# Graph attention and convolution on one core: attention in blocks of a whole pair of heads, with six numerator tiles and an 8-bit mask

## The chip, the cores and the metric

The program runs on one core of one Trainium2 chip. The metric is the device time of that core in microseconds (us). Before the change the median of three runs is 2978.34 us (2978.21 to 2978.59); the profiled execution has a span of 2975.7 us.

## The reference: what is computed

The input `x` holds 32 batches of 512 nodes with 512 features; `adj` is a 512x512 matrix of zeros and ones. Two layers follow each other, each added to its input and normalised per node. The first is attention with 8 heads of 64 features, in which node i sees node j only where `adj` is not zero; the second is a graph convolution with a normalised adjacency.

```python
q = (x @ Wq + bq).reshape(b, n, H, HD)          # the same for k and v
scores = jnp.einsum('bihd,bjhd->bhij', q, k) / jnp.sqrt(jnp.float32(HD))
mask = jnp.where(adj == 0, jnp.float32(-1000000000.0), jnp.float32(0.0))
weights = jax.nn.softmax(scores + mask[None, None, :, :], axis=-1)
out = jnp.einsum('bhij,bjhd->bihd', weights, v)
x = _layernorm(x + out)
norm_adj = adj * deg_inv_sqrt[:, None] * deg_inv_sqrt[None, :]
x = _layernorm(x + norm_adj @ (x @ weight) + bias)
```

## The kernel before, in words

**Attention.** The heads are taken in four pairs g, in the order (0, 2, 1, 3). A step (b, g, jj) handles two of the four 128-row blocks of keys of one pair. `scores` (line 337) multiplies, for each of its two blocks, the keys of both heads with the queries (64 rows of the array per head) into a tile `sc` of PSUM, of which there are two. VectorE then clips and adds the mask (`scalar_tensor_tensor`, line 348) and writes the numerator tile `e`; ScalarE takes its exponential in place (line 351); GpSimd adds the exponentials into `acc`, from which the softmax's denominators come: one addition for jj = 0 and two for jj = 1 (lines 363 to 368). `values` (line 370) multiplies the `e` tiles of a step with the values into `av`, 64 columns of the array per head; after jj = 1 VectorE transposes `av` into `yb` and a DMA puts it into `yT`. `sums` (line 401) adds up `acc` over the partitions on TensorE.

**What runs between.** All other matmuls of a batch are cut into pieces. `seven` (line 250) builds a 1024-wide product from seven pieces of eight matmul instructions each: `values_of` (v0 to v6 below), `keys_and_queries` for r = 0 and r = 1 (q0 to q6, p0 to p6) and, for the second layer, `second` (s0 to s6). `first` makes the four products with the adjacency (f0 to f3). Each piece takes one of three PSUM buffers of `ps_mm`, and VectorE or ScalarE reads it out. Beside them are pieces without matmuls, of cost 0 in the list: `add` (VectorE multiplies a row block of `yT` by the inverse of the denominators, then GpSimd adds the residual), `measure` (VectorE, mean and variance), `root` (GpSimd), `judge` (VectorE), `norm` and `grow` (ScalarE), `split` (VectorE, then GpSimd), `turn` (VectorE transposes x), `combine` (GpSimd, for `xT` and for `parts` of the second layer), `store`.

**The order of the work.** It is written out by hand: every engine gets its instructions in program order (class `InOrder`). The main loop (line 681) runs over steps: scores of step k, values of step k-1, then a share of a list called `side`, made anew per batch at the batch's third step. With eight steps per batch the list of 32 pieces is cut in eighths, four pieces each. For batches 1 to 29 the list is built at lines 696 to 708: the sums' inverse first, then the chain of attention's layer norm (`add`, `measure`, `root`, `judge`, `norm`, `split`, `grow`) woven with what is left of the second layer's norm (`rest`), spread over the pieces v1 to p4; then f0 to f3, `combine` of `parts`, p5, p6, and s0 to s6. `weave` spreads one list over another in equal portions; `run` takes pieces off the front until their cost reaches the share that is due.

So each engine's queue in one eighth is: two score tiles, two value tiles, four pieces on TensorE; two masks, sometimes `yb`, then the pieces' read-outs on VectorE; one or two `acc` additions and then the side list's additions on GpSimd.

Of the kernel before, what the change touches and what calls it, by code (L numbers as in the profile page):

```python
# [8 lines left out]

F32 = mybir.dt.float32  # L10
I32 = mybir.dt.int32
BF16 = mybir.dt.bfloat16
F32R = mybir.dt.float32r
AF = mybir.ActivationFunctionType
ALU = mybir.AluOpType
AX = mybir.AxisListType

P = 128
H = 8
HD = 64  # L20
EPS = 1e-5
MASKED = -1e9
TINY = 1.1754943508222875e-38


CUT = 60.0
# [21 lines left out]
def unshifted(  # L48
# [29 lines left out]
    B, N, D = x.shape  # L78
    NT = N // P
    DT = D // P  # L80
    G = H // 2
# [21 lines left out]
    def load_x(b, j):  # L103


        if b == 0 and j == 1:
            X[b, j] = work.tile([P, 8, DT, 32], F32, name="x1", tag="e", bufs=4)
        else:
            X[b, j] = acts.tile([P, 8, DT, 32], F32, name="x", bufs=1)
        for q in range(4):  # L110
            nc.sync.dma_start(
                X[b, j][32 * q : 32 * (q + 1)],
                x[b, ts(j, HALF), ts(q, P)].rearrange("(k s) (t r) -> s k t r", s=32, r=32),
            )
# [85 lines left out]
    for c in range(2):  # L200
        gpsimd.memset(sel[:, c, c : c + 1], 1.0)
    FINE = consts.tile([P, B], F32, name="fine")
    maskT = consts.tile([P, NT, N], BF16, name="maskT")
    adjT = consts.tile([P, NT, N], F32R, name="adjT")
    dis = consts.tile([P, NT], F32, name="dis")
    lost = consts.tile([P, NT], F32, name="lost")
# [1 line left out]
    def adjacency(m):  # L208


        p = ps_mm.tile([P, N], F32, name="mm")
        for n in range(NT):
            tensor.transpose(p[:, ts(n, P)], adj_sb[:, n, ts(m, P)], ident)
        vector.tensor_scalar(maskT[:, m, :], p, 0.0, MASKED, op0=ALU.is_equal, op1=ALU.mult)
        vector.tensor_copy(adjT[:, m, :], p)
        off = work.tile([P, N], F32, name="off", tag="e", bufs=4)
        vector.tensor_tensor(off, p, adjT[:, m, :], ALU.not_equal)
        vector.tensor_reduce(lost[:, m : m + 1], off, AX.X, ALU.add)

# [117 lines left out]
    def scores(s):  # L337

        b, g, jj = s
        E[s] = [work.tile([P, 2, N], F32, name="e", bufs=4) for _ in range(2)]  # L340
        for l in range(2):
            j = 2 * jj + l
            e = E[s][l]
            p = ps_sc.tile([P, 2, N], F32, name="sc")
            for k in range(2):
                r = slice(k * HD, (k + 1) * HD)
                tensor.matmul(p[:, k, :], KQ[b, g][r, 0, ts(j, P)], KQ[b, g][r, 1, :], start=True, stop=True)
            vector.scalar_tensor_tensor(
                e, p, CUT, maskT[:, j, None, :].to_broadcast([P, 2, N]), op0=ALU.min, op1=ALU.add
            )  # L350
            scalar.activation(e, e, AF.Exp)
        if b == B - 1:

            n = 2 * ORDER.index(g) + jj
            if n == 3:
                a = XT[:, 4:6].rearrange("p k u o -> p k (u o)")
            elif n == 4:
                a = acts.tile([P, 2, N], F32, name="acc4", tag="kq", bufs=5)
            else:
                a = work.tile([P, 2, N], F32, name="acc", bufs=3)  # L360
            ACC.setdefault((b, g), []).append(a)
            gpsimd.tensor_add(a, E[s][0], E[s][1])
        elif jj == 0:
            ACC[b, g] = [work.tile([P, 2, N], F32, name="acc", bufs=3)]
            gpsimd.tensor_add(ACC[b, g][0], E[s][0], E[s][1])
        else:
            for l in range(2):
                gpsimd.tensor_add(ACC[b, g][0], ACC[b, g][0], E[s][l])
# [32 lines left out]
    def sums(b, c):  # L401


        p = ps_mm.tile([P, N], F32, name="mm")
        for q in range(4):
            parts = ACC[b, ORDER[2 * c + q // 2]]
            for k, a in enumerate(parts):
                tensor.matmul(
                    p[32 * q : 32 * (q + 1), :], sel[:, c, :], a[:, q % 2, :],
                    start=k == 0, stop=k == len(parts) - 1,  # L410
                )
        if c == 0:
            SM[b] = work.tile([P, N], F32, name="sT", bufs=1)
            if b < B - 1:
                scalar.copy(SM[b], p)
            else:
                vector.tensor_scalar(SM[b], p, 1e-36, None, op0=ALU.max)
        else:
            vector.scalar_tensor_tensor(SM[b], p, 1e-36, SM[b], op0=ALU.max, op1=ALU.add)
# [111 lines left out]
    def weave(side, main):  # L531

        out, done = [], 0
        for k, piece in enumerate(main):
            due = len(side) * (k + 1) // len(main)
            out += side[done:due] + [piece]
            done = due
        return out + side[done:]
# [109 lines left out]
    def run(pieces, share=1.0):  # L648

        due = share * sum(c for c, _, _ in pieces)  # L650
        done = 0
        while pieces and (done < due or share == 1.0):
            c, f, args = pieces.pop(0)
            f(*args)
            done += c

    ORDER = (0, 2, 1, 3)
    steps = [(b, g, jj) for b in range(B) for g in ORDER for jj in range(2)]
    S = len(steps)
    PER = 2 * G  # L660
    weigh(wv, gpsimd)
    run(sum(turns(0), []))
    weigh(wk, gpsimd)
# [14 lines left out]
    one, two = turns(1)  # L678
    run(one)
    side, rest, held = [], [], None  # L680
    for k in range(S + 2):
        b, at = divmod(k, PER)
        if at == 2:
            run(side)
            if b:
                load_residual(b - 1)
            if b + 2 < B:
                load_x(b + 2, 0)
            if b + 1 < B:
                main, kq = values_of(b + 1) + keys_and_queries(b + 1, 0), keys_and_queries(b + 1, 1)  # L690
                turn0, turn1 = turns(b + 2) if b + 2 < B else ([], [])
                main += kq[:2] + turn0 + kq[2:5]
            if b == 0:
                w1_parts = [(0, weigh_part, (w1, gpsimd, i)) for i in range(4)]
                side = main[:7] + [(0, degrees, ())] + weave(w1_parts, main[7:]) + kq[5:] + turn1
            elif b < B - 1:
                f, c = finish(b - 1), convolve(b - 1)
                norm, split, grow = f["norm"], f["split"], f["grow"]
                chain = f["add"][:1] + rest[:3] + f["add"][1:3] + rest[3:5] + f["add"][3:] + f["measure"][:1] + rest[5:]
                chain += f["measure"][1:] + f["root"] + f["judge"] + norm[:2] + split[:1] + norm[2:3] + split[1:2]  # L700
                chain += norm[3:] + split[2:] + grow
                side = f["inverse"] + main[:1] + weave(chain, main[1:])
                side += c["first"] + c["parts"][:2] + kq[5:6] + c["parts"][2:3] + kq[6:] + turn1[:1]
                if b < B - 2:
                    s = c["second"]
                    side += s[:1] + c["parts"][3:] + s[1:3] + turn1[1:2] + s[3:4] + turn1[2:3] + s[4:5] + turn1[3:4]
                    side += s[5:6] + c["measure"][:1] + turn1[4:] + s[6:] + c["measure"][1:2]
                    rest = c["measure"][2:] + c["root"] + c["store"]
                else:
                    side += c["parts"][3:]  # L710
                    held = c
            else:
                f, c = finish(b - 1), convolve(b - 1)
                s, norm, split = held["second"], f["norm"], f["split"]
                side = s[:1] + f["inverse"] + s[1:2] + f["add"][:2] + s[2:3] + f["add"][2:] + s[3:4] + f["measure"][:2]
                side += s[4:5] + f["measure"][2:] + f["root"] + s[5:6] + f["judge"] + held["measure"][:2] + s[6:]
                spread = norm[:2] + held["measure"][2:3] + split[:1] + norm[2:3] + held["measure"][3:] + split[1:2]
                spread += held["root"] + norm[3:] + split[2:] + held["store"]
                side += [(0.5, *piece[1:]) for piece in spread] + c["first"] + c["parts"] + f["grow"]
        if k >= 2:  # L720
            pb, pg, pj = steps[k - 2]
            if pj == 1 and pg in ORDER[1::2]:
                sums(pb, ORDER.index(pg) // 2)
        if k < S:
            scores(steps[k])
        if k == 0:
            run(two)
        if 1 <= k <= S:
            values(steps[k - 1])
        if k == S - 4:  # L730
            load_residual(B - 1)
            last = finish(B - 1)
        if k == S - 1:
            run(last["early"])
        run(side, 1.0 / (PER - (at - 2) % PER))
    run(side)

    f, e = last, convolve(B - 1)
    s, norm, split, block, add = c["second"], f["norm"], f["split"], e["block"], f["late"][1:]
# [308 lines left out]
```

## Time and profile before

| | busy us | share of the span | instructions |
|---|---|---|---|
| TensorE matmul | 2910.5 | 98% | 12966 |
| VectorE | 2110.8 | 71% | 2908 |
| ScalarE | 1064.8 | 36% | 1342 |
| GpSimd | 1827.4 | 61% | 1141 |

The largest groups of the profile, with the number of instructions and the mean duration: the mask on VectorE, 512 of 1217 ns; the exponential on ScalarE, 512 of 1057 ns; additions into `acc` on GpSimd, 248 of 2457 ns (onto `acc`) and 131 of 2438 ns (of two `e` tiles); score matmuls, 2048 of 618 ns; value matmuls, 2048 of 609 ns. The durations of matmuls overlap each other, so the distance from one start to the next says more than a duration. A busy share of 98% on TensorE means that a matmul is nearly always in flight, not that every start follows the last as soon as it could. A "wait" names the engine whose instruction came last before the waiting one could start. Idle time of an engine that doesn't set the end costs nothing.

### The profile page before, as it was taken

The numbers are of one execution on the slowest core, as the hardware profiler recorded it, in microseconds if no ns is written. First come the engines' busy times: TensorE is split into PE (matmuls) and PEld (weight loads), VectorE is DVE, ScalarE is ACT, GpSimd is POOL, SyncE is SP. The second block draws the span as 40 slices with busy tenths as digits, with TensorE's granted clock in tenths as the row PEclk, the third lists the DMA queues.
The fourth block names the chain that finished last, engine by engine and source line by source line (L and its number), as shares of the span: only waits on it lengthen the run. The fifth ranks groups of instructions, "written<-read, shape, count | busy, mean of one in ns | idle before, by whom it ended". The sixth has DMA issues, their size and how long they took to land.

```text
span 2975.7 us, 35550 instructions
## 1 busy us (share of the span) xinstructions
PE 2910.5 (98%) x12966; PEld 1865.2 (63%) x12966; DVE 2110.8 (71%) x2908; ACT 1064.8 (36%) x1342; POOL 1827.4 (61%) x1141
## 2 busy tenths in 40 slices
PE   7999999999999999999999999999999999999997
PEld 5666666666666666666666666666666666666645
DVE  6667766677666777666777667776667766677766
ACT  1233323343333433333433333433344333333333
POOL 2656666666666566666666665666666666666655
PEclk9999999999999999999999999999999999999998
DMA  5111121212112111211121121112111211121111
GB/s 128 33 25 47 47 57 39 49 40 54 47 47 49 41 46 47 57 39 44 44 56 47 46 47 43 46 47 55 41 40 46 57 46 47 46 43 47 42 40 51
DMA packets 383399, 142.41 MB, mean 48 GB/s; under 512 B 280048, under 2 KB 349680, under 8 KB 383216
## 3 DMA queue, kind: packets, MB, share of 16 engines
q1 hardware_dynamic: 381920, 138.75, 19.6%
q8 instruction: 104, 1.70, 0.2%
q10 hardware_dynamic: 1296, 1.31, 0.2%
q14 instruction: 79, 0.65, 0.1%
HBM read 72.88 MB, written 33.55 MB: 36 GB/s over the span
## 4 chain that ended last, share of the span: by engine, by line
PE 66%; DVE 17%; POOL 7%; issue 6%; DMA 1%; ACT 1%; SPq 0%; DVEq 0%; POOLq 0%; ACTq 0%
PE mm L42 44%; PE sc L42 12%; PE av L42 10%; DVE e L42 6%; POOL acc L42 5%; DVE yT L42 3%; DVE st L42 2%; DVE y L42 2%; DVE v L42 1%; POOL xT L42 1%; ACT e L42 1%; POOL y L42 1%; DMA xr<-in_x_dram 1%; DVE u L42 1%; DVE yb L42 1%
## 5 line engine op out<-in xcount | busy, mean ns | idle before, releaser
L42 ACT ACTIVATE e<-e 128x1024 f32<-128x1024 f32 x512 | 541.2, 1057 | 1230.7 <-DVE e L42 1211.7
L42 POOL TENSOR_TENSOR acc<-acc,e 128x1024 f32<-128x1024 f32 x248 | 609.2, 2457 | 400.2 <-ACT e L42 390.5
L42 DVE SCALAR_TENSOR_TENSOR e<-sc,maskT 128x1024 f32<-128x1024 f32 x512 | 601.8, 1217 | 111.5 <-PE sc L42 99.4
L42 POOL TENSOR_TENSOR acc<-e 128x1024 f32<-128x1024 f32 x131 | 319.4, 2438 | 408.0 <-ACT e L42 408.0
L42 PE MATMUL sc<-kq 64*128 64x512 f32 x2048 | 512.0, 618 | 5.4 <-DVE e L42 5.4
L42 PE MATMUL av<-e,v 128*64 128x512 f32 x2048 | 499.6, 609 | 5.2 <-DVE yb L42 3.5
L42 PE MATMUL mm<-xT,wk 128*128 128x256 f32 x1792 | 475.4, 388 | 23.1 <-DVE e L42 22.2
L42 PE MATMUL mm<-xT,wq 128*128 128x256 f32 x1792 | 460.0, 379 | 0.0
L42 PEld LDWEIGHTS mm<-xT,wk 128*128 128x128 f32 x1792 | 327.9, 190 | 174.6 <-DVE e L42 51.1
L42 PE MATMUL mm<-wv,xT 128*128 128x256 f32 x1792 | 405.8, 384 | 12.8 <-DVE xT L42 10.8
L42 PEld LDWEIGHTS mm<-wv,xT 128*128 128x128 f32 x1792 | 338.7, 192 | 84.1 <-DVE u L42 22.7
L42 PEld LDWEIGHTS mm<-xT,wq 128*128 128x128 f32 x1792 | 341.0, 190 | 45.4
L42 PEld LDWEIGHTS av<-e,v 128*64 128x64 f32 x2048 | 124.9, 137 | 348.3 <-issue 339.2
L42 PEld LDWEIGHTS sc<-kq 64*128 64x128 f32 x2048 | 177.0, 187 | 246.5 <-issue 233.2
L42 DVE TENSOR_TENSOR kq<-u,mm 128x512 f32<-128x512 f32 x128 | 87.8, 686 | 250.8 <-PE mm L42 247.8
L42 PE MATMUL mm<-w,zT 128*128 128x256 f32 x1024 | 232.4, 380 | 0.6 <-DVE zT L42 0.6
L42 DVE TENSOR_TENSOR yT<-yT,inv 128x512 f32<-128x512 f32 (+1 forms) x140 | 230.1, 1669 | 0.1
L42 PEld LDWEIGHTS mm<-w,zT 128*128 128x128 f32 x1024 | 194.3, 190 | 28.8 <-DVE zT L42 1.0
L42 PE MATMUL mm<-adjT,hi 128*128 128x512 f32 x496 | 205.1, 413 | 0.0
L42 POOL TENSOR_TENSOR yT<-yT,b_r 128x512 f32<-128x512 f32 x128 | 188.2, 1490 | 25.3 <-DVE lo L42 25.3
L42 PE MATMUL mm<-adjT,lo 128*128 128x512 f32 x496 | 196.5, 396 | 0.8 <-DVE lo L42 0.8
L42 DVE TENSOR_TENSOR y<-y,mm 128x512 f32<-128x512 f32 x160 | 106.0, 680 | 125.6 <-POOL y L42 75.7
(103 smaller groups left out, 3112.1 us busy)
## 6 DMA issues: line engine op xcount, KB each, us to landing
x<-in_x_dram SPq DMA_DIRECT2D x256, 128.0 KB, 3.0
yT<-yb SPq DMA_DIRECT2D x512, 64.0 KB, 2.5
out_dram<-y SPq DMA_DIRECT2D x128, 256.0 KB, 2.1
xr<-in_x_dram SPq DMA_DIRECT2D x124, 256.0 KB, 3.4
wv<-in_L_gnn_Wv_dram ACTq DMA_DIRECT2D x8, 128.0 KB, 5.0
wk<-in_L_gnn_Wk_dram SPq DMA_DIRECT2D x8, 128.0 KB, 4.2
wq<-in_L_gnn_Wq_dram SPq DMA_DIRECT2D x8, 128.0 KB, 4.7
yT<-in_adj_dram SPq DMA_DIRECT2D x1, 1024.0 KB, 6.8
```

Source lines behind the costliest of these rows:

```text
L42: return self.tc.keep_in_program_order(op(*args, **kwargs))
```

## The change

It has four parts.

1. The loop runs over blocks of a whole pair of heads (four per batch) in place of half pairs. In a block TensorE makes the scores of the pair's first half, then all values of the pair in front, then (in every second block) `sums`, then the scores of the second half, and then a quarter of the side list in one go. The additions into `acc` are taken out of `scores` into `accumulate`: that of the first half comes after `sums`, those of the second half after its scores.
2. Six numerator tiles `e` in place of four, since four of a pair are kept while two of the next are made. Two `acc` tiles in place of three, and other spare places for the last batch.
3. The mask is kept as bytes, 255 where there is no edge, and subtracted; before it was 16-bit, -1e9, and added. The score is clipped at 60, so a masked numerator is exp of at most -195, zero in 32 bits. This frees the room for part 2.
4. The chain of attention's layer norm comes later in the side list: `rest` is woven over the first five pieces, and the chain, with the inverse, over the fifteen that follow.

```diff
-        E[s] = [work.tile([P, 2, N], F32, name="e", bufs=4) for _ in range(2)]
+        E[s] = [work.tile([P, 2, N], F32, name="e", bufs=6) for _ in range(2)]
...
-                e, p, CUT, maskT[:, j, None, :].to_broadcast([P, 2, N]), op0=ALU.min, op1=ALU.add
+                e, p, CUT, maskT[:, j, None, :].to_broadcast([P, 2, N]), op0=ALU.min, op1=ALU.subtract
...
-                chain = f["add"][:1] + rest[:3] + f["add"][1:3] + rest[3:5] + f["add"][3:] + f["measure"][:1] + rest[5:]
-                chain += f["measure"][1:] + f["root"] + f["judge"] + norm[:2] + split[:1] + norm[2:3] + split[1:2]
-                chain += norm[3:] + split[2:] + grow
-                side = f["inverse"] + main[:1] + weave(chain, main[1:])
+                chain = f["inverse"] + f["add"] + f["measure"] + f["root"] + f["judge"] + norm[:2] + split[:1]
+                chain += norm[2:3] + split[1:2] + norm[3:] + split[2:] + grow
+                side = weave(rest, main[:5]) + weave(chain, main[5:])
...
-        if k >= 2:
-            pb, pg, pj = steps[k - 2]
-            if pj == 1 and pg in ORDER[1::2]:
-                sums(pb, ORDER.index(pg) // 2)
         if k < S:
-            scores(steps[k])
+            scores((*blocks[k], 0))
+        if k:
+            values((*blocks[k - 1], 0))
+            values((*blocks[k - 1], 1))
+            if k % 2 == 0:
+                sums(blocks[k - 1][0], (k - 1) % G // 2)
+        if k < S:
+            accumulate((*blocks[k], 0))
+            scores((*blocks[k], 1))
+            accumulate((*blocks[k], 1))
         if k == 0:
             run(two)
-        if 1 <= k <= S:
-            values(steps[k - 1])
...
-        run(side, 1.0 / (PER - (at - 2) % PER))
+        run(side, 1.0 / (G - (at - 1) % G))
```

More of the change, by code (lines that the diff above doesn't have):

```diff
@@ L11 @@
 I32 = mybir.dt.int32
-BF16 = mybir.dt.bfloat16
+U8 = mybir.dt.uint8
 F32R = mybir.dt.float32r
@@ L22 @@
 MASKED = -1e9
+FAR = 255.0
 TINY = 1.1754943508222875e-38
@@ L106, in load_x @@
         if b == 0 and j == 1:
-            X[b, j] = work.tile([P, 8, DT, 32], F32, name="x1", tag="e", bufs=4)
+            X[b, j] = work.tile([P, 8, DT, 32], F32, name="x1", tag="e", bufs=6)
         else:
@@ L202, in unshifted @@
     FINE = consts.tile([P, B], F32, name="fine")
-    maskT = consts.tile([P, NT, N], BF16, name="maskT")
+    maskT = consts.tile([P, NT, N], U8, name="maskT")
     adjT = consts.tile([P, NT, N], F32R, name="adjT")
@@ L213, in adjacency @@
             tensor.transpose(p[:, ts(n, P)], adj_sb[:, n, ts(m, P)], ident)
-        vector.tensor_scalar(maskT[:, m, :], p, 0.0, MASKED, op0=ALU.is_equal, op1=ALU.mult)
+        vector.tensor_scalar(maskT[:, m, :], p, 0.0, FAR, op0=ALU.is_equal, op1=ALU.mult)
         vector.tensor_copy(adjT[:, m, :], p)
-        off = work.tile([P, N], F32, name="off", tag="e", bufs=4)
+        off = work.tile([P, N], F32, name="off", tag="e", bufs=6)
         vector.tensor_tensor(off, p, adjT[:, m, :], ALU.not_equal)
@@ L348, in scores, with accumulate @@
             vector.scalar_tensor_tensor(
-                e, p, CUT, maskT[:, j, None, :].to_broadcast([P, 2, N]), op0=ALU.min, op1=ALU.add
+                e, p, CUT, maskT[:, j, None, :].to_broadcast([P, 2, N]), op0=ALU.min, op1=ALU.subtract
             )
             scalar.activation(e, e, AF.Exp)
+    def accumulate(s):
+        b, g, jj = s
+        n = 2 * ORDER.index(g) + jj
+        a = None
         if b == B - 1:
[L354 to L360, printed above, removed]
+            if n in (2, 6, 7):
+                a = XT[:, 0:2] if n == 7 else XT[:, 4:6]
+                a = a.rearrange("p k u o -> p k (u o)")
+            elif n == 3:
+                a = acts.tile([P, 2, N], F32, name="acc3", tag="kq", bufs=5)
+        if a is None and (jj == 0 or b == B - 1):
+            a = work.tile([P, 2, N], F32, name="acc", bufs=2)
+        if a is not None:
             ACC.setdefault((b, g), []).append(a)
             gpsimd.tensor_add(a, E[s][0], E[s][1])
-        elif jj == 0:
-            ACC[b, g] = [work.tile([P, 2, N], F32, name="acc", bufs=3)]
-            gpsimd.tensor_add(ACC[b, g][0], E[s][0], E[s][1])
         else:
@@ L657, in unshifted @@
     ORDER = (0, 2, 1, 3)
-    steps = [(b, g, jj) for b in range(B) for g in ORDER for jj in range(2)]
-    S = len(steps)
-    PER = 2 * G
+    blocks = [(b, g) for b in range(B) for g in ORDER]
+    S = len(blocks)
     weigh(wv, gpsimd)
@@ L680, in unshifted @@
     side, rest, held = [], [], None
-    for k in range(S + 2):
-        b, at = divmod(k, PER)
-        if at == 2:
+    for k in range(S + 1):
+        b, at = divmod(k, G)
+        if at == 1:
             run(side)
@@ L719, in unshifted @@
                 side += [(0.5, *piece[1:]) for piece in spread] + c["first"] + c["parts"] + f["grow"]
-        if k >= 2:
-            pb, pg, pj = steps[k - 2]
-            if pj == 1 and pg in ORDER[1::2]:
-                sums(pb, ORDER.index(pg) // 2)
         if k < S:
-            scores(steps[k])
+            scores((*blocks[k], 0))
[8 more added lines that the diff above has]
+            accumulate((*blocks[k], 1))
         if k == 0:
             run(two)
-        if 1 <= k <= S:
-            values(steps[k - 1])
-        if k == S - 4:
+        if k == S - 2:
             load_residual(B - 1)
@@ L734, in unshifted @@
             run(last["early"])
-        run(side, 1.0 / (PER - (at - 2) % PER))
-    run(side)
+        run(side, 1.0 / (G - (at - 1) % G))
     f, e = last, convolve(B - 1)
```

## The prediction, before the result was known

> **What bounds the kernel now.** I read the page first, for the engine that sets the end.
>
> ```profile
> PE 2910.5 (98%) x12966; PEld 1865.2 (63%) x12966; DVE 2110.8 (71%) x2908; ACT 1064.8 (36%) x1342; POOL 1827.4 (61%) x1141
> PE 66%; DVE 17%; POOL 7%; issue 6%; DMA 1%; ACT 1%; SPq 0%; DVEq 0%; POOLq 0%; ACTq 0%
> ```
>
> TensorE (PE) is nearly never without a matmul. Next, its own waits: only one repeats, 29 times, once per full batch.
>
> ```profile
> PE mm L42 <- DVE e L42: 24.2, 29, 2.0
> ```
>
> The third view is the timeline of TensorE in mid-run (start, length of the group, name):
>
> ```profile
> 1527.01 1.99 PE L42 MATMUL sc<-kq 64*128 64x512 f32 x8
> 1528.93 1.94 PE L42 MATMUL av<-e,v 128*64 128x512 f32 x8
> 1530.79 1.13 PE L42 MATMUL mm<-xT,wk 128*128 128x256 f32 x4
> 1531.76 1.03 PE L42 MATMUL mm<-xT,wq 128*128 128x256 f32 x4
> 1532.62 1.03 PE L42 MATMUL mm<-xT,wk 128*128 128x256 f32 x4
> ...
> 1537.90 1.06 PE L42 MATMUL mm<-acc,sel 128*32 128x512 f32 x8
> ```
>
> From 1531.76 to 1532.62 four matmuls take 0.864, so 0.216 each, 1.728 per piece of eight. The four pieces from 1530.79 to 1537.90 take 7.10, not 32 x 0.216 = 6.91: 0.19 is lost. Scores run in pairs of starts 0.43 apart, so 4 x 0.43 = 1.72, but values start 1.92 after scores: 0.20 lost. Values to the next group: 1.87, 0.15 lost. Each turn scores, values, pieces loses 0.54 to three changes of the array's shape (64*128, 128*64, 128*128).
>
> The fourth view shows what the other engines do to each other: VectorE (DVE) and GpSimd (POOL) around the repeating wait.
>
> ```profile
> 1518.05 2.35 DVE L42 SCALAR_TENSOR_TENSOR e<-sc,maskT 128x1024 f32<-128x1024 f32 x2
> 1520.32 3.46 DVE L42 TENSOR_TENSOR yT<-yT,inv 128x512 f32<-128x512 f32 x2
> 1523.69 0.68 DVE L42 TENSOR_TENSOR v<-u,mm 128x512 f32<-128x512 f32 x1
> 1524.29 0.68 DVE L42 TENSOR_TENSOR e<-e,mm 128x512 f32<-128x512 f32 x1
> 1520.49 5.49 POOL L42 TENSOR_TENSOR acc<-acc,e 128x1024 f32<-128x1024 f32 x2 [2.31 <-ACT e L42]
> 1525.11 1.10 PE L42 MATMUL mm<-xT,wk 128*128 128x256 f32 x4 [0.79 <-DVE e L42]
> ```
>
> Two multiplications of `add` need 3.46: the first 0.6, the second only after GpSimd's first addition to acc. v4's read-out comes late (1524.97), its PSUM buffer is wanted by q0 at 1518.87 + 0.10 + 3 x 1.728 = 1524.15, and q0 starts at 1525.11: 0.95 lost per batch.
>
> **The Trainium skill.** "TensorEngine Tiling (Array Packing)", Key Properties, says that changing the tiling mode, not just the tile, drains TensorE. The trace agrees: 0.15 to 0.20 at each change, none within a mode. "SBUF — State Buffer", Who interferes with whom, says that a VectorE instruction with two SBUF inputs contends with GpSimd's reads, and one with a single SBUF input does not. The trace agrees: `add` took up to 2.86 us beside acc and 0.68 without, while the mask (scores in PSUM) stays at 1.14 from start to start.
>
> **The change, part by part.**
>
> *Blocks of a pair: fewer changes of shape.* Before, a pair had 2 x (pieces to scores + scores to values + values to pieces). Entry and exit can be told apart by the first start-to-start time of a group: pieces enter 0.10 late (1530.79 to 1531.76 is 0.97, not 0.864) and leave 0.09 late; scores enter 0.10 late (their weight loads at 1503.81 and 1504.34 lie 0.53 apart, not 0.43) and leave 0.10 late; values 0.05 and 0.10. So, to three places, 0.197, 0.148 and 0.204; a pair pays 1.098. After: pieces to scores 0.197, scores to values 0.148, values to scores, scores to pieces. The trace has no undisturbed values-to-scores; I bound it by the cheapest and dearest change, 0.148 to 0.204, and take 0.198 (exit 0.094 to 0.10, entry of scores 0.104). Scores to pieces: exit 0.097 + entry 0.104 = 0.201. Sum 0.744; saved 0.354 (0.348 to 0.398), times 128 pairs 45.3 us. `inverse`'s transposes (shape of the pieces) stood right behind values and paid the entry there; in mid-list they save nothing: 31 x 0.1 = 3.1 back. Saving 42.2.
>
> *The old wait goes.* The adds now come after v5, behind which acc is long done: 29 x 0.95 = 27.6 saved.
>
> *Longer runs, and both acc additions in front.* Cutting the list (67.8 of cost; 2.1 per piece, 0.6 the inverse) in quarters gives: Q1 v0-v4, inverse, v5, add0, add1, v6, add2, q0; Q2 add3, m0, q1, m1, q2, m2, m3, q3, root, q4, judge, q5, q6, split0, p0, split1, p1 (norms between); Q3 norm3, split2, turn, split3, p2, p3, p4, f0-f3, two parts, p5; Q4 the third part, p6, s0-s6. Let T be the quarter's first matmul. The second scores start at T - 1.92; the first mask 1.25 later (1527.01 to 1528.26), at T - 0.67, the second at T + 0.47; VectorE is free at T + 1.60. The exponential follows 1.25 after its mask and takes 1.06; so acc's first addition is due at T + 1.72, and two take until about T + 6.9. Everything of the side list on GpSimd queues behind that. Three places where TensorE then waits:
>
> - Q2: add3's multiplication goes first (T + 1.60 to 2.28; acc then T + 1.77 to 4.49 and 4.52 to 6.88); its GpSimd addition (1.27) ends at T + 8.12. VectorE gets to m3 by T + 5.85 (add3 0.59, three measures of 0.82, q1 and q2 of 0.60) and waits; m3 ends at 9.02, q3's read-out (0.37 + 0.47) at 9.86; 0.14 later its buffer is free. q6 wants it at T + 0.10 + 5 x 1.728 = 8.74. Wait 1.26.
> - Q3: split2 (0.62), turn (1.17), split3 blocked by acc until T + 4.4, then 0.6; p2's read-out ends at T + 5.72, its buffer is free at 5.87; f0 wants it at T + 0.10 + 3 x 1.728 = 5.28. Wait 0.58.
> - Q4: the third part's subtraction follows acc (4.08, 6.52) and ends at T + 7.77; s3 needs it at T + 0.10 + 4 x 1.728 = 7.01, starts at 7.87. Wait 0.86. Before, one acc addition stood ahead of it, and s3 came an eighth later.
>
> Sum 2.70 per batch, 29 batches: 78.3 added. I find no wait in Q1, nor of second scores: their PSUM needs the first mask done 5.5 us after the first scores start, and the latest I get is 3.6 (after Q2, where p1's read-out waits for ScalarE's norms).
>
> *Costed at nothing.* Byte mask: no row has a byte operand. The nearest is the same instruction with a 32-bit second operand (sT, 692 ns for 512 elements); the mask, 16-bit, takes 1217 for 1024, that is 1.03 ns for each further element, so the width shows nothing, and I take bytes at 1217 too. Were they a tenth dearer, 4 x 0.12 us per pair would lie in VectorE's idle share (29%). Six e tiles: a mask waits for values and acc of three half pairs ago, done. Two acc tiles: the first half's addition waits for sums, ends by T + 0.6, before acc's next at T + 1.72. Later chain: behind it f0 needs lo by T + 6.9, it is there at 5.0. Start and last batch have the same work in other lumps; waits there moved by up to 8 us either way, taken as 0.
>
> Sum: 2978.3 - 42.2 - 27.6 + 78.3 = 2986.8.
>
> **The rivals.** *Forecast:* new waits eat the saving, 2987.
> *B, faster:* Q3's and Q4's waits are hidden (an acc addition that starts earlier by half a microsecond does it), only Q2's is left, 29 x 1.26 = 36.5: 2978.3 - 42.2 - 27.6 + 36.5 = 2945. For it: margins of 0.6 to 0.9 us on a walk of some 8 us. Against: the walk uses this trace's own start-to-start times. With no wait at all: 2908.
> *C, slower still:* at T + 1.6 VectorE's two-input instruction and acc race for the SBUF port, 0.12 us apart. If acc wins in Q3, split2, turn and split3 are pushed behind both additions, p2's read-out ends near T + 8.6, and f0 waits 3.5 in place of 0.58: 29 x 2.9 = 85 more, 3072. At 1520.32 and 1554.33 VectorE won.
> *D, even:* waits of 2.4 per batch, 2978.
>
> **How the numbers follow.** Forecast 0.43, B 0.35, D 0.13, C 0.09. Predicted 2987. Low 2925 takes in B and half of the way to no wait; high 3040 takes in waits a half larger (2.70 to 4.05 is 39 us) and stops short of most of C. Faster by over 0.2% (6 us): B, 0.35. Same: D, 0.13. Slower: forecast and C, 0.52.
>
> **What would show it.** Right: TensorE's waits name VectorE before q6 (kq buffers) and f0, and GpSimd before s3, each some 29 times, 1.3, 0.6 and 0.9; q0's wait gone; the period of a batch, 91.07 now (from one q0 wait to the next), at 91.5 (91.07 - 4 x 0.354 + 0.10 - 0.95 + 2.70); values to second scores 0.2 above 3.43. Wrong: a period near 90, if those waits are absent; shape changes that cost nothing when values precede scores; waits of second scores on the mask, which I cost at nothing; a mask above 1.22 us.

## The result, and the profile after

| | before | after |
|---|---|---|
| median, us | 2978.47 | 2992.16 (2991.76 to 2992.61) |
| span of the profiled execution, us | 2975.7 | 2990.2 |
| TensorE busy, us | 2910.5 | 2880.3 |
| VectorE busy, us | 2110.8 | 1982.2 |
| one batch (from its first score matmul to the next batch's), us | 91.07 | 91.48 |

The ratio after to before is 1.0046, with a 95% interval of 1.0029 to 1.0064: slower by 13.7 us. The prediction was 2987, slower by 8.5.

The engine totals of the page after:

```profile
PE 2880.3 (96%) x12966; PEld 1879.2 (63%) x12966; DVE 1982.2 (66%) x2908; ACT 1062.9 (36%) x1342; POOL 1807.1 (60%) x1141
```

Two things can be misread here. TensorE is busy for 30 us *less* while the span grows by 14.5: a drain between two shapes of the array counts as busy, as matmuls are still in flight, and a wait doesn't. And VectorE has the same 2908 instructions but is busy for 129 us less; this comes back at the end. The page's chain of waits holds nothing this time but the last ScalarE instruction (0% of the span), so it can't be used; TensorE's own waits can.

TensorE's waits after (who waits, for whom: us in total, times, longest):

```profile
PE mm L44 <- DVE u L44: 29.5, 29, 1.0
PE mm L44 <- POOL parts L44: 20.4, 29, 1.0
PE mm L44 <- DVE e L44: 12.2, 32, 2.0
```

In place of one wait per batch there are three. `u` is q3's read-out (q6 waits for its buffer), `parts` the third subtraction (s3 waits for it), and most of `e` is p2's read-out (f0 waits for its buffer). The totals count only the time after the modelled end of the matmul in flight. From start to start q6 comes 1.18 us late, s3 0.86, f0 about 0.6. Those of s3 and f0 in mid-run (the subtraction or the read-out, then TensorE's first matmul that waited for it):

```profile
1497.07 1.26 POOL L44 TENSOR_TENSOR parts<-zT 128x512 f32<-128x512 f32 x1
1498.38 2.00 PE L44 MATMUL mm<-w,parts 128*128 128x256 f32 x8 [0.69 <-POOL parts L44]
...
1471.98 0.68 DVE L44 TENSOR_TENSOR e<-e,mm 128x512 f32<-128x512 f32 x1
1472.71 0.50 PE L44 MATMUL mm<-adjT,hi 128*128 128x512 f32 x1 [0.26 <-DVE e L44]
```

For q6, the timeline of the second quarter of a batch, T = 1444.28, answers the third and fourth view of before. TensorE:

```profile
1442.36 1.99 PE L44 MATMUL sc<-kq 64*128 64x512 f32 x8
1444.28 1.13 PE L44 MATMUL mm<-xT,wk 128*128 128x256 f32 x4
...
1454.21 1.13 PE L44 MATMUL mm<-xT,wk 128*128 128x256 f32 x4 [1.03 <-DVE u L44]
```

VectorE and GpSimd over the same stretch:

```profile
1445.88 0.68 DVE L44 TENSOR_TENSOR yT<-yT,inv 128x512 f32<-128x512 f32 x1
1452.48 0.69 DVE L44 BATCH_NORM_STATS2 st<-yT 128x6 f32<-128x512 f32 x1 [2.30 <-POOL yT L44]
1453.31 0.84 DVE L44 SCALAR_TENSOR_TENSOR u<-e,step,mm 128x256 f32<-128x256 f32 x2
...
1446.06 5.16 POOL L44 TENSOR_TENSOR acc<-acc,e 128x1024 f32<-128x1024 f32 x2 [1.14 <-ACT e L44]
1451.17 1.28 POOL L44 TENSOR_TENSOR yT<-yT,xr 128x512 f32<-128x512 f32 x1
```

add3's multiplication runs at T + 1.60. Its GpSimd addition stands behind both additions into acc and ends at T + 8.17. m3 waits 2.30 for it, q3's read-out stands behind m3 and ends at T + 9.87, and q6 starts at T + 9.93. The prediction had 1.60, 8.12, 9.86 and 10.0.

The shape changes can be read from TensorE's starts in mid-run:

```profile
1459.58 1.99 PE L44 MATMUL sc<-kq 64*128 64x512 f32 x8
1461.50 3.65 PE L44 MATMUL av<-e,v 128*64 128x512 f32 x16
1465.09 1.99 PE L44 MATMUL sc<-kq 64*128 64x512 f32 x8
1467.00 1.13 PE L44 MATMUL mm<-xT,wk 128*128 128x256 f32 x4
```

Split into what a group loses at its first step and at its last one, as the prediction did, a pair now pays 0.197 (pieces to scores), 0.148 (scores to values), 0.204 (values to scores) and 0.201 (scores to pieces), 0.750 in all against 1.098. Values to scores had only been bounded; it costs the upper end of its bounds, 0.204.

Where the 14.5 us of the span are, from the start of the same score matmul in both traces: the changed kernel is 4.35 us ahead at the start of batch 2 (1.7 of it because eight more value matmuls are still to come), falls back by 0.41 per batch (11.5 over 28 batches), by 2.9 in batch 30, and by 4.5 in the last batch and after it. Batch 30's list is cut elsewhere: one piece more of 1.9 us, f0, falls into it, and a wait of 1.2. In the last batch the longest wait for `lo` is 6.5 in place of 0.8.

### The profile page after: what moved, and what is told of

Read it like the earlier page. It is cut to its first block, busy times and chain, and to the rows that moved or that the text cites. A ratio compares the mean times of both kernels' runs of the same rounds, so it can differ in the third digit from the quotient of the medians.

```text
span 2990.2 us, 35412 instructions
## 1 busy us (share of the span) xinstructions
PE 2880.3 (96%) x12966; PEld 1879.2 (63%) x12966; DVE 1982.2 (66%) x2908; ACT 1062.9 (36%) x1342; POOL 1807.1 (60%) x1141
## 3 DMA queue, kind: packets, MB, share of 16 engines
q10 hardware_dynamic: 1296, 1.31, 0.2%
## 5 line engine op out<-in xcount | busy, mean ns | idle before, releaser
L44 POOL TENSOR_TENSOR acc<-acc,e 128x1024 f32<-128x1024 f32 x248 | 620.0, 2500 | 158.1 <-ACT e L44 148.2
L44 DVE SCALAR_TENSOR_TENSOR e<-sc,maskT 128x1024 f32<-128x1024 f32 x512 | 601.9, 1217 | 120.3 <-PE sc L44 120.2
L44 POOL TENSOR_TENSOR acc<-e 128x1024 f32<-128x1024 f32 x129 | 303.3, 2351 | 557.9 <-PE mm L44 312.4
L44 PE MATMUL av<-e,v 128*64 128x512 f32 x2048 | 469.8, 601 | 0.0
L44 PEld LDWEIGHTS av<-e,v 128*64 128x64 f32 x2048 | 136.1, 137 | 317.8 <-issue 315.7
L44 POOL TENSOR_TENSOR yT<-yT,xr 128x512 f32<-128x512 f32 (+1 forms) x128 | 180.7, 1431 | 137.4 <-DVE yT L44 128.5
L44 DVE STREAM_TRANSPOSE yb<-av 128x512 f32<-128x512 f32 x128 | 91.7, 717 | 224.9 <-PE av L44 217.2
L44 POOL TENSOR_TENSOR yT<-yT,b_r 128x512 f32<-128x512 f32 x128 | 163.6, 1288 | 100.2 <-DVE lo L44 99.5
```

Source lines behind the costliest of these rows:

```text
L44: return self.tc.keep_in_program_order(op(*args, **kwargs))
```

## The experiments

The theory: fewer shape changes save 1.3 us per batch and the old wait 0.95, and three new waits take back 2.7, because both additions into acc now stand ahead of a whole quarter's GpSimd work, and because of the order of VectorE's queue. The main rival: a run of eight pieces is too dense for VectorE, so that a wait taken away at one piece comes back at the next. Ratios are to the kernel before, with 95% intervals.

**The byte mask alone.** The kernel before with part 3 only:

```diff
-    maskT = consts.tile([P, NT, N], BF16, name="maskT")
+    maskT = consts.tile([P, NT, N], U8, name="maskT")
...
-                e, p, CUT, maskT[:, j, None, :].to_broadcast([P, 2, N]), op0=ALU.min, op1=ALU.add
+                e, p, CUT, maskT[:, j, None, :].to_broadcast([P, 2, N]), op0=ALU.min, op1=ALU.subtract
```

> The kernel before with the byte mask alone (255, subtracted), half pairs and four numerator tiles as before. Theory (new waits eat what fewer shape changes save): the mask costs nothing, 1217 ns per mask as now, 2978.5 us within 1 us. Rival (the byte operand is dearer and VectorE's read-outs come late): mask above 1.25 us and 2985 us or more.

Measured 2978.19 us, ratio 1.000 (0.9992 to 1.0009). The group of the mask:

```profile
L43 DVE SCALAR_TENSOR_TENSOR e<-sc,maskT 128x1024 f32<-128x1024 f32 x512 | 601.7, 1217 | 111.4 <-PE sc L43 99.4
```

1217 ns as with 16 bits, and 1217 in the changed kernel too. The mask is free.

**The later layer norm alone.** The kernel before with part 4 only:

```diff
-                side = f["inverse"] + main[:1] + weave(chain, main[1:])
+                side = weave(rest, main[:5]) + weave(chain, main[5:])
```

(With the chain of the change.)

> The kernel before with the later layer norm alone (the inverse and the chain behind the fifth piece), half pairs as before. Theory: the one wait of before (q0 for v4's read-out, 0.95 us in 28 batches) goes and no other comes, as each eighth has room for its chain: 2978.5 - 27 = 2952 us. Rival (a denser chain makes VectorE late wherever it stands): the wait moves to another piece, 2978 us or more.

Measured 2950.14 us, ratio 0.9906 (0.9889 to 0.9923). No repeating wait is left, and a batch takes 90.05: 1.02 less. On half pairs this part is worth 28 us.

**The blocks with the early layer norm.** The changed kernel without part 4: the diff above, the other way.

> The changed kernel with the early layer norm of before. Theory: all four adds then lie in the first quarter, ahead of the next acc additions, so q6's wait (1.18 us) goes; add0 now meets acc in the first quarter and v4's read-out comes late, q0 waits some 0.8 us; f0 and s3 wait as before: 2992 - 29 x 0.4 = 2981 us, and 3 less for the inverse at the head of the list: 2978 us. Rival (length of the uninterrupted run of pieces is what makes VectorE late): q6's wait stays and q0's comes on top, 3015 us.

Measured 2955.64 us, ratio 0.9922 (0.9905 to 0.9938): 22 us faster than expected, and 36.5 faster than the changed kernel. q6's wait is gone, f0 and s3 wait as before, a batch takes 90.21; the expected wait of q0 isn't there. VectorE in the first quarter, T = 1496.23:

```profile
1499.26 1.65 DVE L44 TENSOR_TENSOR yT<-yT,inv 128x512 f32<-128x512 f32 x1
...
1505.69 1.29 DVE L44 TENSOR_TENSOR yT<-yT,inv 128x512 f32<-128x512 f32 x2
1506.90 0.68 DVE L44 TENSOR_TENSOR v<-u,mm 128x512 f32<-128x512 f32 x1
1507.50 0.68 DVE L44 TENSOR_TENSOR e<-e,mm 128x512 f32<-128x512 f32 x1
```

add0 was blocked by acc, as expected, but add1 and add2 ran in 1.29 together, with GpSimd between two instructions. v4's read-out ended at T + 11.95, before q0 wants its buffer at T + 12.6. So each of the two parts is a gain by itself (22 and 28 us), and together they are a loss: on blocks, the later chain puts add3 behind the acc additions.

**Halves in turn.** Inside a block scores, values, scores, values:

```diff
             values((*blocks[k - 1], 0))
+        if k < S:
+            scores((*blocks[k], 1))
+        if k:
             values((*blocks[k - 1], 1))
...
             accumulate((*blocks[k], 0))
-            scores((*blocks[k], 1))
             accumulate((*blocks[k], 1))
```

> The changed kernel with scores and values of the halves in turn inside a block (scores, values, scores, values, then the quarter of the list): as many shape changes as before, all else as changed. Theory: 0.354 us more in each of 128 pairs, 45 us: 2992 + 45 = 3037 us, and up to 10 us either way because acc's additions start at another time against the pieces. Rival (shape changes are not what a block saves): within 10 us of 2992.

Measured 3077.67 us, ratio 1.0335 (1.0317 to 1.0352), 85 above the changed kernel. The expectation miscounted: this order has five changes of shape per pair, before six, after four, so one more is paid, 0.15 x 4 = 0.60 us per batch. The batch takes 94.41, 2.93 more. The rest, 2.3 us, is in the three waits: q6 comes 1.75 late in place of 1.18, s3 1.71 in place of 0.86, f0 about 0.9 later than it did. For f0, VectorE shows why (T = 1417.39):

```profile
1417.51 0.72 DVE L44 STREAM_TRANSPOSE yb<-av 128x512 f32<-128x512 f32 x1 [0.37 <-PE av L44]
1418.15 2.46 DVE L44 SCALAR_TENSOR_TENSOR lo<-yT,dis,hi 128x512 fp32r<-128x512 f32 x1
1420.53 1.23 DVE L44 STREAM_TRANSPOSE xT<-x 128x1024 f32<-128x1024 f32 x1
1421.69 1.68 DVE L44 SCALAR_TENSOR_TENSOR lo<-yT,dis,hi 128x512 fp32r<-128x512 f32 x1
```

`yb` now stands ahead of split2, acc's addition is already running (from 1417.69), and split2 takes 2.46 in place of 0.74. That is close to the prediction's case C, but VectorE is held up by the first of the two additions only, and f0 comes some 1.5 us late, not 3.5. As a price of shape changes the run is not clean; the direct reading above is.

**add3 ahead of q0.**

```diff
-                side = weave(rest, main[:5]) + weave(chain, main[5:])
+                woven = weave(chain, main[5:])
+                woven.insert(6, woven.pop(7))
+                side = weave(rest, main[:5]) + woven
```

> The changed kernel with one piece of the list moved by one place: add3 stands ahead of q0, so it falls into the first quarter and its GpSimd addition ahead of the next acc additions. Theory: m3 no longer waits for it, q3's buffer comes free in time, q6's wait of 1.18 us goes in 29 batches, all else stays: 2992 - 34 = 2958 us. Rival (VectorE has too much to do in a long run of pieces): the wait stays or moves, 2985 us or more.

Measured 2956.31 us, ratio 0.9927 (0.991 to 0.9943). One piece without a matmul, moved by one place, is worth 36 us. The line of `DVE u` is gone from TensorE's waits, the other two stay.

**The third part ahead of p5.**

```diff
-                side += c["first"] + c["parts"][:2] + kq[5:6] + c["parts"][2:3] + kq[6:] + turn1[:1]
+                side += c["first"] + c["parts"][:3] + kq[5:6] + kq[6:] + turn1[:1]
```

> The changed kernel with the third subtraction of parts (GpSimd alone) moved ahead of p5, so out of the fourth quarter into the third. Theory: s3's wait of 0.85 us goes in 29 batches: 2992 - 25 = 2967 us. Rival (VectorE's backlog sets the pace): no change, since VectorE's queue is the same, 2990 us or more.

Measured 2963.98 us, ratio 0.9954 (0.9938 to 0.9971), 28 less than the changed kernel. VectorE's queue is untouched here, so this wait was one for GpSimd's order, against the rival.

**p2 ahead of split3, the transpose behind p3.** To `woven` of the run with add3, in place of its move:

```diff
+                    woven.insert(29, woven.pop(31))
+                    woven.insert(34, woven.pop(30))
```

> The changed kernel with p2 between split2 and split3, and the transpose of x behind p3: the same work, but p2's read-out no longer stands behind the transpose and the blocked split3. Theory: f0's wait of 0.6 us goes in 28 or 29 batches: 2992 - 17 = 2975 us. Rival (f0 waits for the lo of split3, or for the port, not for p2's buffer): 2990 us or more.

Measured 3064.56 us, ratio 1.0287 (1.027 to 1.0304): far off. f0 starts in time. But f2 now waits, 29 times:

```profile
PE mm L44 <- ACT zT L44: 55.4, 29, 1.9
```

ScalarE's timeline there:

```profile
1417.96 0.72 ACT L44 ACTIVATE yT<-yT,rdeg 128x512 f32<-128x512 f32 x1 [3.20 <-POOL yT L44]
1419.19 0.72 ACT L44 ACTIVATE yT<-yT,rdeg 128x512 f32<-128x512 f32 x1 [0.51 <-POOL yT L44]
1419.82 1.06 ACT L44 COPY zT<-mm 128x512 f32<-128x512 f32 x2
```

f0's copy stands behind grow2 and grow3, which wait for GpSimd's additions behind acc. In the changed kernel f3 is the piece that takes f0's buffer; in this one it is f2, one piece earlier (here f2's first matmul waits for ScalarE's semaphore, there f3's does). Why the buffers are handed out in another order was not tried. The wait costs more than itself, as the windows around two of them show (us of the window; busy us and instructions of TensorE, its weight loads, VectorE, ScalarE, GpSimd; granted TensorE clock; DMA):

```profile
1418.00:1435.00 17.00, 15.12 (x69) 7.61 (x68) 5.61 (x7) 5.65 (x8) 5.89 (x4) 1.00 0.15 31
1511.00:1528.00 17.00, 15.09 (x63) 8.16 (x63) 4.33 (x5) 5.69 (x8) 4.35 (x5) 0.90 0.11 25
```

In about every second batch the granted clock is 0.90 over such a window, and the batch takes 94.67 in place of 93.13. The trace's record of the clock shows where that comes from. It stands at 0.50 for 3.41 us, and at 1.00 before and after; all such stretches of this run begin whole multiples of 3.41 us apart, as on a grid. Here are two neighbouring cells of this grid for each of the same two waits:

```profile
1511.29:1514.70 3.41, 1.50 (x7) 0.95 (x6) 0.00 (x0) 2.21 (x4) 1.00 (x1) 1.00 0.48 109
1514.70:1518.11 3.41, 3.41 (x10) 2.63 (x9) 0.00 (x0) 0.59 (x1) 0.00 (x0) 0.50 0.00 0
1415.72:1419.13 3.41, 2.83 (x13) 1.94 (x11) 1.80 (x3) 0.72 (x1) 3.41 (x3) 1.00 0.46 118
1419.13:1422.54 3.41, 2.10 (x9) 1.74 (x10) 0.00 (x0) 1.68 (x3) 0.03 (x1) 1.00 0.18 38
```

The first wait lies in one cell (TensorE idle for 1.91 us of it), and the next cell has half the clock. The second is split over two cells (0.58 and 1.31), and the clock stays. Between 250 and 2800 us this run and the next one have 55 such waits. In the 37 with at least 1.90 us of idle time in one cell the clock fell, in the 18 with at most 1.89 it did not (idle time by the modelled ends of the matmuls). So it is the wait's place on the grid that picks the batches.

**All three moves.**

> The changed kernel with all three moves. Theory: the three waits add up, since each stands in a quarter of its own: 2992 - 77 = 2915 us, and TensorE is left with the waits of the start and the last batch. Rival (the work of a quarter is too dense for VectorE, and a wait taken away at one piece comes back at another): 2950 us or more.

Measured 3010.8 us, ratio 1.0109 (1.0092 to 1.0126). The waits of q6 and s3 are gone, f2's is the same as in the run before (57.3 us in 29). A batch takes 92.49, or 90.95 where the clock is granted in full. So the move of the transpose, not the adding up of the moves, is what failed; the run with p2 as well, below, differs from this one in that move alone and takes 87 us less.

**add3 and the third part.** The two diffs that paid.

> The changed kernel with the two moves that paid: add3 ahead of q0, and the third subtraction of parts ahead of p5. Theory (waits in different quarters add up): the batch's period falls from 91.48 by 1.22 and 0.96 us, as it did with each alone, to 89.30: 2992 - 63 = 2929 us. Rival (a wait taken away comes back elsewhere in the batch): 2945 us or more.

Measured 2928.68 us, ratio 0.9836 (0.9819 to 0.9852), a batch 89.30, exactly as added up from the two alone. The rival falls: two waits were taken away and neither came back.

**p2 as well, the transpose left ahead of split3.**

```diff
+                if b + 2 < B:
+                    woven.insert(29, woven.pop(31))
```

> As the run with add3 and the part ahead, and p2's read-out between split2 and the transpose of x, which stays ahead of split3. Theory of f0's wait: f0 waits for p2's buffer, so its 0.6 us go; but f0's copy stays behind grow2 and grow3 on ScalarE, which wait for GpSimd's additions behind acc, and f3 wants f0's buffer about 0.4 us before that copy ends: net 0.2 us per batch, 2929 - 5 = 2924 us. Rival (buffers are handed out in another order, as when the transpose stood behind p3): f2 waits 2 us for f0's copy, 2990 us. Rival (f0's wait was the blocked split3): 2929 us.

Measured 2923.61 us, ratio 0.9818 (0.9802 to 0.9835), a batch 89.09. f0's wait is gone; 0.2 us of the 0.6 are gained, as f3, which takes f0's buffer, now starts 0.27 late.

**grow2 and grow3 behind f1.**

```diff
+                woven = [piece for piece in woven if piece not in grow[2:]]
...
-                side += c["first"] + c["parts"][:3] + kq[5:6] + kq[6:] + turn1[:1]
+                side += c["first"][:2] + grow[2:] + c["first"][2:] + c["parts"][:3] + kq[5:6] + kq[6:] + turn1[:1]
```

> As the run before it, and grow2 and grow3 (ScalarE) behind f1, so that f0's copy waits for nothing on GpSimd. Theory: no repeating wait of TensorE is left, the period is 91.48 - 1.22 - 0.96 - 0.6 = 88.7: 2992 - 80 = 2912 us; against the half-pair kernel with the later norm alone (period 90.05, no repeating wait either) this shows the price of the shape changes alone, 4 x 0.35 - 0.1 = 1.3 us per batch. Rival: a wait comes back elsewhere, 2920 us or more.

Measured 2911.2 us, ratio 0.9777 (0.9761 to 0.9793), a batch 88.71. The part that had been lost again at f3 is gained too. TensorE's waits of 2 us and more in total:

```profile
PE mm L44 <- DMA wv<-in_L_gnn_Wv_dram: 9.6, 1, 9.6
PE mm L44 <- DVE lo L44: 8.0, 3, 6.2
PE sc L44 <- DVE e L44: 7.7, 2, 4.8
PE sc L44 <- ACT hi L44: 5.4, 1, 5.4
PE mm L44 <- DVE e L44: 3.7, 3, 1.4
```

All of the start and of the last two batches. Against the half pairs with no repeating wait (90.05) a batch is 1.34 us shorter, which is what the blocks themselves are worth; 1.32 was predicted.

**The last batch.**

```diff
-        if k == S - 1:
-            run(last["early"])
         run(side, 1.0 / (G - (at - 1) % G))
+        if k == S - 1:
+            run(last["early"])
```

> As the run with no repeating waits, and in the last batch the first half of the last layer norm's multiplications (eight on VectorE, 4.9 us in a row) behind the last but one share of the list in place of ahead of it. In the changed kernel they stand ahead of the split that the adjacency product waits 6.5 us for. Theory: most of that wait goes, 5 us less, 2907 us. Rival (it is only put off to the last share): no change within 2 us.

Measured 2908.7 us, ratio 0.9767 (0.9751 to 0.9783), 2.5 us under the run before, with intervals that overlap. The wait of 6.2 us for `lo` became three of 1.3 to 2.2 us, 5.2 us in all in place of 8.0: half of what was expected, and not a clear gain. It is 2.3% faster than the kernel before, 2.8% faster than the changed one (2908.7 / 2992.2).

## Why the prediction was right

The time came out 5 us above the forecast, with the same sign and by the mechanism given.

- *Fewer changes of shape*: 0.354 saved per pair predicted, 0.348 read from the trace. As a difference of two kernels without repeating waits, 1.34 per batch against 1.32. Two small errors cancel here: the inverse's transposes, with the losses around them, take 0.59 behind values (before) and 0.63 in mid-list (after), so they give back 0.05 per batch, not 0.10. One sign was ill put: values to second scores is some 0.15 above 3.43 (3.59 in the lines above), not 0.2, since part of that change's price shows only behind the first scores.
- *The old wait*: gone, as predicted. The half-pair kernel with the later norm shows its size, 1.02 per batch against 0.95. It occurs 28 times, not 29 (one of the 29 on its line is a wait of 2.0 at the start). The blocks with the early norm don't have it either, so on blocks the later chain was not needed for this.
- *The three new waits*: q6 1.18 (predicted 1.26), f0 about 0.6 (0.58), s3 0.86 (0.86). Taken away one after the other they gave 1.22, 0.96 and 0.59, in sum 2.77 per batch against 2.70. The walk left out that a late start loses another 0.10 at the second matmul (s3's and q6's come 0.32 after the first, within a run of pieces 0.22; at the old wait it was 0.29). For f0 there was luck: it could have started at T + 5.09, as it does without a wait, not 5.28, and its buffer was free at T + 5.7, not 5.87; the two errors cancel.
- *A batch*: 91.48 against 91.5.
- *Costed at nothing*: the byte mask is shown to be. Second scores don't wait in mid-run, as predicted. Six numerator tiles and two acc tiles were not tried alone; no repeating wait of TensorE has been traced to them. GpSimd's first addition into acc does wait for `sums`, 62 times, and ends by T + 0.65, as predicted, ahead of the next at T + 1.78.
- *Start and last batch*, taken as 0 within 8 us: they gave 4.4 and took 7.4, so they cost 3. The forecast's sum had about 3.5 saved outside the 28 batches in the middle (four batches with fewer shape changes, 5.3, less the waits of one more batch, 1.75). In the middle it was right (11.5 measured, 12.0 forecast), so this is where forecast and result part.
- Rival B, at 0.35, needed the margins of 0.6 to 0.9 us to vanish; none did. Case C didn't happen in the changed kernel; with the halves in turn VectorE lost to one addition, not to two.

What the forecast left out is that the slow part was cheap to mend. It named the queue behind acc and stopped there; the same walk, asked which piece should have stood ahead of it, gives add3 and the third part at once.

## What to carry to other kernels

Where several in-order engines share one hand-written list, a coarser cut changes what stands ahead of what: put down for each queue what the new order places in front, from measured start-to-start times, and look for the buffer that comes free too late. That walk gave waits right to 0.1 us here (one of them with luck), where busy shares (71% and 61%) showed neither VectorE nor GpSimd near its bound. Judge two edits together as well as alone: the later norm and the blocks gained 28 and 22 us apart and lost 14 together, and the loss was mended by giving a few pieces another place on VectorE, ScalarE and GpSimd, with TensorE's own order untouched.

## What the runs showed of the hardware that was not expected

- A wait of TensorE of 1.9 us can halve its clock for the 3.41 us that follow on the clock's grid, which costs 1.5 us more each time (94.67 against 93.13 for a batch). It did so in 37 of 55 such waits, exactly those with 1.90 us or more of idle time inside one cell of the grid. Shorter waits never did: 1.0 us of idle time for q6 in the changed kernel, 1.6 with the halves in turn (both 0.994 over the span).
- VectorE's busy time includes its time blocked by GpSimd. The same 124 multiplications by `inv` took 1796 ns on average before and 828 after, `judge`'s two-input instruction on 32 elements 2145 and 225. It goes the other way too: 31 additions of `eps` to four numbers took 202 ns before and 2038 after, where they start beside the additions into acc and end with them (1425.78 to 1428.01; the two additions run from 1423.19 to 1427.99). In sum these three make up about 125 of the 129 us that VectorE lost in busy time, and the span grew all the same.
